# A sorting network on VectorE: every fifth large compare-exchange gets its minimum from integer sums on GpSimd, gathers are issued between the steps, and the closing linear layer runs for four tiles at once on TensorE

## The chip, the cores and the metric

The kernel runs on one core of a Trainium2 chip, in one launch. The metric is the device time of one execution in microseconds (us). One execution was also taken by the hardware profiler; every duration of a single instruction below comes from it.

## What is computed

Two graph layers run one after the other. The first is an attention layer over 4096 nodes and a sparse adjacency matrix; the change doesn't touch it. The second gathers, for every node, the feature rows (128 numbers) of the neighbours that are kept, sorts them feature by feature, takes three quantiles of each feature, and ends in a linear layer:

```python
vals = jnp.where(keep[:, :, None], x[None, :, :], big)
svals = jnp.sort(vals, axis=1)
...
for q in QUANTILES:                       # 0.25, 0.5, 0.75
    idx = jnp.maximum(jnp.ceil(q * n_keep).astype(jnp.int32) - 1, 0)
    picked = jnp.take_along_axis(svals, idx[:, None, None], axis=1)[:, 0, :]
    agg = agg + w_q * picked              # w_q = 1/3
...
agg = 0.5 * agg + 0.5 * x
out = agg @ W.T + b + x
```

## The kernel before

**Two stages.** The first 3850 us are the attention layer (`gat`). Then `sparse` (L1516) does the second layer, and this is the stage that is changed. It goes through 32 tiles of 128 nodes, one node to a partition, ordered by their number of kept neighbours: tile t has `HIGH[t]` = 50 to 100 slots, each a row of 128 float32 of one neighbour.

**One tile.** `load` (L1653) issues from GpSimd's queue (POOL) one indirect DMA for the node's list of neighbours (`info`), one for its own features (`xs`) and one for each slot (`gather`, L1548, whose DMA is L1549), so some 66 for a usual tile. They fill one of three buffers `rows`, so the gathers of tile t+1 can only begin when the quantiles of tile t-2 have been read out of theirs. `plan` (L1500) makes a sorting network for the slots, cut down to the positions that the quantiles need, and `steps` packs equal compare-exchanges into rectangles of at most 16 slots (`PAIRS`), that is 2048 numbers per partition. The network of a tile is done in two halves: the first half beside the second half of the tile before it. `interleave` (L1467) merges the two lists so that neighbouring steps touch different slots.

**One step.** `compare` (L1572) of a step that needs both results copies the low side with ScalarE (ACT) to a tile of PSUM (`low`, two buffers; `low_s` in SBUF for up to four slots), and VectorE (DVE) then writes the minimum over the low side and the maximum over the high side:

```python
nc.scalar.copy(packed, lows)                                     # L1583
nc.vector.tensor_tensor(lows, packed, highs, op=ALU.min)         # L1584
nc.vector.tensor_tensor(highs, packed, highs, op=ALU.max)        # L1585
```

Steps that need one result take one DVE instruction (L1587, L1589).

**The end of a tile.** `finish` (L1591) reads out the three quantiles with weights (L1618 to L1632) into `agg`; the largest tiles have extra slots that are merged here (L1599 to L1614). Then DVE adds `agg` and `xs` and halves them (L1636, L1637), TensorE transposes the tile (L1639), ACT copies it, TensorE multiplies it with the weights (L1642), DVE adds `xs`, the bias and the product (L1644, L1645), and an indirect DMA on POOL's queue writes the tile (L1646).

**What sets the order.** The Tile framework decides where instructions stand on each engine when the program is built; from then on every engine takes its own list strictly in order, and an instruction that waits for a semaphore holds up all behind it. POOL's list in this stage holds nothing but the indirect DMAs.

Of the kernel before, what the change touches and what calls it, by code (L numbers as in the profile page):

```python
# [38 lines left out]
F32 = mybir.dt.float32  # L39
F16 = mybir.dt.float16  # L40
BF = mybir.dt.bfloat16
I32 = mybir.dt.int32
# [3 lines left out]
ALU = mybir.AluOpType  # L46
# [4 lines left out]
P = 128  # L51
N = 4096
D = 128
# [34 lines left out]
MAIN = 64  # L88
PAIRS = 16
SMALL = 4  # L90

BLOCKS = (4, 4, 6, 6, 6, 6)
START = tuple(sum(BLOCKS[:b]) for b in range(len(BLOCKS)))
# [1373 lines left out]
def interleave(jobs):  # L1467


    at, last, now = [0] * len(jobs), {}, 0  # L1470
    left = [list(j) for j in jobs]
    while any(left):
        best = None
        for j, todo in enumerate(left):
            seen = set()
            for i, step in enumerate(todo[:24]):
                if not (step[-1] & seen):
                    since = now - max((last.get((j, x), -9) for x in step[-1]), default=-9)
                    rank = (min(since, 3), -j, -i)
                    if best is None or rank > best[0]:  # L1480
                        best = (rank, j, i)
                seen |= step[-1]
        _, j, i = best
        step = left[j].pop(i)
        for x in step[-1]:
            last[j, x] = now
        now += 1
        yield j, step


def places(t):
# [24 lines left out]
def sparse(tc, nc, c, x1_d, meta_d, order_d, w, b, out):  # L1516


    with tc.tile_pool(name="sp1", bufs=1) as one, tc.tile_pool(
# [3 lines left out]
    ) as psum:  # L1523
        w_sb = one.tile([P, D], F32, name="lw")
        nc.scalar.dma_start(out=w_sb, in_=w)
        bbc = one.tile([P, D], F32, name="lb")
        nc.scalar.dma_start(out=bbc, in_=b.partition_broadcast(P))
        wT = one.tile([P, D], F32, name="lwT")
        it = one.tile([P, 2 * MIDDLE], I32, name="it_p")
        nc.gpsimd.iota(it, pattern=[[1, 2 * MIDDLE]], base=0, channel_multiplier=0)  # L1530
# [4 lines left out]
        for i in range(4):  # L1535
            nc.sync.dma_start(
                out=order[:, ts(i, NT // 4)],
                in_=order_d[ts(i, N // 4), :].rearrange("(t p) c -> p (t c)", p=P),
            )

        def bank():
            return psum.tile([P, PAIRS * D], F32, name="low")
# [5 lines left out]
        def gather(row, info, col):  # L1548
            nc.gpsimd.indirect_dma_start(  # L1549
                out=row,  # L1550
                out_offset=None,
                in_=x1_d,
                in_offset=bass.IndirectOffsetOnAxis(ap=info[:, col : col + 1], axis=0),
            )

        def view(t, at, *dims):

            dims = [[x * D, k] for x, k in dims if k > 1]
            return bass.AP(
                tensor=t.tensor, offset=t.offset + at * D, ap=[list(t.ap[0]), *dims, [1, D]]  # L1560
            )

        def block(t, shape, shift=0):
            s, n2, step2, n, step, run = shape
            dims = [[x * D, k] for x, k in ((step2, n2), (step, n)) if k > 1]
            return bass.AP(
                tensor=t.tensor,
                offset=t.offset + (s + shift) * D,
                ap=[list(t.ap[0]), *dims, [1, run * D]],
            )  # L1570

        def compare(rows, step):  # L1572
            shape, d, low, high, _ = step
            lows, highs = block(rows, shape), block(rows, shape, d)
            if low and high:
                _, n2, _, n, _, run = shape
                k = n2 * n * run
                if k > SMALL:
                    t = bank()
                else:  # L1580
                    t = tp.tile([P, SMALL * D], F32, name="low_s", bufs=4)
                packed = block(t, (0, n2, n * run, n, run, run))
# [3 lines that stand above are left out]
            elif low:  # L1586
                nc.vector.tensor_tensor(lows, lows, highs, op=ALU.min)  # L1587
            else:
                nc.vector.tensor_tensor(highs, lows, highs, op=ALU.max)  # L1589

        def finish(t, rows, xs, info, extra):  # L1591
            agg = tp.tile([P, D], F32, name="agg")
            shift = MIDDLE - HIGH[t] // 2
            for q, (lo, hi) in enumerate(places(t)):
                n = hi - lo + 1
                if extra:
                    cut = one.tile([P, 3 * (80 - MAIN) * D], F32, name="cut")
                    grid = view(cut, 0, (extra, n), (1, extra))
                    nc.vector.tensor_tensor(  # L1599
                        grid,  # L1600
                        view(rows, lo - extra - 1, (1, n), (1, extra)),
                        view(rows, MAIN, (0, n), (1, extra)),
                        op=ALU.max,
                    )
                    m = extra
                    while m > 1:
                        h = m // 2
                        a = view(cut, 0, (extra, n), (1, h))
                        nc.vector.tensor_tensor(
                            a, a, view(cut, m - h, (extra, n), (1, h)), op=ALU.min  # L1610
                        )
                        m -= h
                    best = view(rows, lo - 1, (1, n))
                    nc.vector.tensor_tensor(best, best, view(cut, 0, (extra, n)), op=ALU.min)  # L1614
                if q == 0:
                    begun = False
                weight = tp.tile([P, 8], F32, name="weight", bufs=4)
                nc.vector.tensor_scalar(  # L1618
                    weight[:, :n],
                    iota_p[:, lo + shift : hi + 1 + shift],  # L1620
                    info.bitcast(F32)[:, POS + q : POS + q + 1],
                    third,
                    op0=ALU.is_equal,
                    op1=ALU.mult,
                )
                for i in range(n):
                    v = view(rows, lo - 1 + i)
                    if not begun:
                        nc.vector.tensor_scalar(agg, v, weight[:, i : i + 1], None, op0=ALU.mult)
                        begun = True  # L1630
                    else:
                        nc.vector.scalar_tensor_tensor(  # L1632
                            agg, v, weight[:, i : i + 1], agg, op0=ALU.mult, op1=ALU.add
                        )
            com = tp.tile([P, D], F32, name="com")
            nc.vector.tensor_add(com, agg, xs)  # L1636
            nc.vector.tensor_scalar(com, com, 0.5, None, op0=ALU.mult)  # L1637
            ps = bank()
            nc.tensor.transpose(ps[:, :P], com, c["idf"])  # L1639
            comT = tp.tile([P, P], F32, name="comT")  # L1640
            nc.scalar.copy(comT, ps[:, :P])
            nc.tensor.matmul(ps[:, 512 : 512 + D], comT, wT, start=True, stop=True)  # L1642
            o = tp.tile([P, D], F32, name="o", bufs=4)
            nc.vector.tensor_add(o, xs, bbc)  # L1644
            nc.vector.tensor_add(o, o, ps[:, 512 : 512 + D])  # L1645
            nc.gpsimd.indirect_dma_start(  # L1646
                out=out,
                out_offset=bass.IndirectOffsetOnAxis(ap=info[:, NODE : NODE + 1], axis=0),
                in_=o,
                in_offset=None,  # L1650
            )

        def load(t):  # L1653
            rows = three.tile([P, max(HIGH), D], F32, name="rows")
            xs = three.tile([P, D], F32, name="xs")
            info = three.tile([P, MW], I32, name="info", bufs=4)
            nc.gpsimd.indirect_dma_start(
                out=info,
                out_offset=None,
                in_=meta_d,  # L1660
                in_offset=bass.IndirectOffsetOnAxis(ap=order[:, t : t + 1], axis=0),
            )
            gather(xs, info, NODE)
            for s in range(HIGH[t]):
                gather(rows[:, s, :], info, s)
            return rows, xs, info

        plans = [plan(t) for t in range(NT)]
        held = {0: load(0), 1: load(1)}
        for t in range(NT + 1):  # L1670
            if 0 < t < NT - 1:
                held[t + 1] = load(t + 1)
            jobs = [
                plans[t - 1][1] if t > 0 else [],
                plans[t][0] if t < NT else [],
            ]
            for j, step in interleave(jobs):
                compare(held[t - 1 + j][0], step)
            if t > 0:
                finish(t - 1, *held.pop(t - 1), plans[t - 1][2])  # L1680


def kept(tc, nc, c, adj, kt_d, num, s2):
# [401 lines left out]
```

## Time and profile before

| | |
|---|---|
| median of 11 runs | 8641.98 us (8606.69 to 8652.89) |
| the profiled execution | 8628.19 us, its span 8626.4 us |
| the sorting stage, 3850 to 8575 us of the span | 4725 us |
| in it busy: DVE | 4343.53 us |
| in it busy: POOL | 2145.52 us |
| in it busy: ACT | 1684.47 us |
| in it busy: PE | 39.37 us |

A busy time is the sum over an engine's instructions. Groups of instructions are listed by line, engine, operation and tile, with their count, busy time, mean duration in ns, and the idle time of the engine just before them with what ended it. The timeline lists single instructions with their start.

### The profile page before, as it was taken

To read this page: it belongs to the slowest core of one execution; us is meant where nothing else is said; L and a number is where in the kernel's file an instruction comes from. 1 tells how busy PE (TensorE), PEld (TensorE's weight loads), DVE (VectorE), ACT (ScalarE), POOL (GpSimd) and SP (SyncE) were. 2 spreads that over 40 slices of the span, in tenths; PEclk is the share of its full clock that TensorE was granted. 3 is DMA by queue.
4 is the path that set the end of the run, shared out by engine and by line. 5 is a ranking of instruction groups with operands and counts; after the bars stand their busy time and mean duration, and the time that the engine had idled before them with its cause. 6 is when DMAs were issued, how large, how long until landed. Compare 5 with 4: busy or idle time off the path is not lost. (4 is left out here: it accounts for less than half of the span.)

```text
span 8626.4 us, 29926 instructions
## 1 busy us (share of the span) xinstructions
PE 1162.3 (13%) x5587; PEld 954.8 (11%) x5587; DVE 5920.5 (69%) x9452; ACT 2153.1 (25%) x2120; POOL 4412.7 (51%) x4564
## 2 busy tenths in 40 slices
PE   3122232322233333330000000000000000000000
PEld 1122222212122222220000000000000000000000
DVE  6344544535432222226988999999989999999999
ACT  5011211200000000002333333333333333333333
POOL 1666566555666666656554454453545355453510
PEclk5565656656565665565555555555555555555555
DMA  5232322222122222211111111110111011110100
GB/s 178 45 87 64 80 67 68 79 45 46 44 42 48 50 49 50 49 40 42 35 37 32 27 36 31 29 40 25 38 28 36 22 31 33 27 38 23 36 8 1
DMA packets 222575, 385.09 MB, mean 45 GB/s; under 512 B 121637, under 2 KB 133416, under 8 KB 222376
## 3 DMA queue, kind: packets, MB, share of 16 engines
q0 software_dynamic: 145664, 305.55, 15.2%
q1 hardware_dynamic: 64258, 70.19, 2.7%
q10 hardware_dynamic: 12454, 7.34, 0.3%
q14 instruction: 153, 1.25, 0.1%
q8 instruction: 46, 0.75, 0.0%
HBM read 372.47 MB, written 10.31 MB: 44 GB/s over the span
## 5 line engine op out<-in xcount | busy, mean ns | idle before, releaser
L1549 POOL DMA_INDIRECT rows<-x_d,info x2078 | 2043.1, 983 | 2065.1 <-DVE agg L1632 1049.9
L886 POOL DMA_INDIRECT nb<-xf_d,ids x2250 | 2140.1, 951 | 1285.6 <-issue 655.0
L1583 ACT COPY low<-rows 128x2048 f32<-128x2048 f32 (+9 forms) x1009 | 1548.2, 1551 | 2563.3 <-DVE rows L1585 1711.3
L1584 DVE TENSOR_TENSOR rows<-low,rows 128x2048 f32<-128x2048 f32 (+9 forms) x1009 | 1878.2, 1886 | 208.9 <-issue 92.8
L1585 DVE TENSOR_TENSOR rows<-low,rows 128x2048 f32<-128x2048 f32 (+9 forms) x1009 | 1876.4, 1885 | 4.2 <-DVE rows L1584 1.2
L1008 PE MATMUL ps_z<-spread,nb 128*128 128x128 f32 x4500 | 782.9, 334 | 1375.9 <-issue 591.1
L1008 PEld LDWEIGHTS ps_z<-spread,nb 128*128 128x128 f32 x4500 | 724.5, 245 | 1472.1 <-issue 909.9
L1001 DVE TENSOR_TENSOR spread<-e,ps_small 128x1152 f32<-128x1152 f32 (+4 forms) x312 | 342.6, 1108 | 735.0 <-remote 643.1
L1639 PE MATMUL low<-idf,com 128*128 128x128 f32 x32 | 15.2, 474 | 4716.7 <-issue 2420.3
L1639 PEld LDWEIGHTS low<-idf,com 128*128 128x128 f32 x32 | 5.8, 182 | 4726.1 <-issue 2425.0
L970 ACT ACTIVATE ps_e<-e 128x256 f32<-128x256 f32 (+4 forms) x64 | 26.1, 408 | 1643.2 <-DVE e L962 981.5
L1646 POOL DMA_INDIRECT out<-o,info x32 | 39.8, 1244 | 503.5 <-DVE o L1645 488.8
L182 DVE MAX8 lists<-cand 128x8 f32<-128x176 f32 x416 | 131.4, 334 | 177.1 <-remote 117.3
L1583 ACT COPY low_s<-rows 128x256 f32<-128x256 f32 (+3 forms) x321 | 144.7, 470 | 398.9 <-issue 140.5
L367 ACT ACTIVATE nz<-a_i 128x1024 bf16<-128x1024 int32 x128 | 134.3, 1049 | 369.5 <-remote 287.3
L182 DVE MAX8 k<-key 128x8 f32<-128x256 f32 x416 | 167.8, 415 | 77.2 <-remote 55.0
L950 DVE TENSOR_REDUCE den<-ps_e 128x32 f32<-128x256 f32 (+15 forms) x92 | 30.4, 356 | 236.3 <-ACT ps_e L982 188.2
L900 DVE TENSOR_TENSOR mine<-me,group 128x64 f32<-128x64 f32 x32 | 6.8, 213 | 258.8 <-remote 163.5
L1585 DVE TENSOR_TENSOR rows<-low_s,rows 128x256 f32<-128x256 f32 (+3 forms) x321 | 157.2, 499 | 4.5 <-DVE rows L1584 3.3
L1584 DVE TENSOR_TENSOR rows<-low_s,rows 128x256 f32<-128x256 f32 (+3 forms) x321 | 156.9, 499 | 1.4 <-ACT low_s L1583 0.7
L184 DVE MATCH_REPLACE8 key<-k,key 128x256 f32<-128x256 f32 x384 | 156.4, 409 | 0.0
L962 DVE TENSOR_TENSOR e<-nb,ps_small 128x144 f32<-128x144 f32 (+8 forms) x166 | 39.9, 260 | 164.6 <-DMA nb<-xf_d,ids 152.8
(222 smaller groups left out, 2592.1 us busy)
## 6 DMA issues: line engine op xcount, KB each, us to landing
a_i<-in_adj SPq DMA_DIRECT2D x128, 512.0 KB
nb<-xf_d,ids POOLq DMA_INDIRECT x2250
rows<-x_d,info POOLq DMA_INDIRECT x2078
xf_d<-xf ACTq DMA_DIRECT2D x4, 576.0 KB
xf<-in_x ACTq DMA_DIRECT2D x4, 512.0 KB
meta_d<-rowdata_k SPq DMA_DIRECT2D x4, 324.0 KB
abc_ta<-in_L_gnn_a ACTq DMA_DIRECT2D x2, 512.0 KB
w_ga<-in_L_gnn_W ACTq DMA_DIRECT2D x2, 512.0 KB
```

The lines of the kernel that those rows point to most:

```text
L182: nc.vector.max(out=top, in_=work)
L184: nc.vector.match_replace(out=work, in_to_replace=top, in_values=work, imm_value=gone)
L367: nc.scalar.activation(nz[:, j, :], a_i, AF.Relu, scale=-1.0, accum_out=self.negative[:, k : k + 1],)
L886: gather = nc.gpsimd.indirect_dma_start(out=rows[:, at + i, :], out_offset=None, in_=xf_d, in_offset=bass.IndirectOffsetOnAxis(ap=ids[:, k ...
L962: nc.vector.tensor_tensor(by_group(e, (g, m, r[g], at)), by_group(rows[:, :, D:], (g, m, r[g], k)), of_group(f1, (g, m, r[g], at)), op=ALU ...
L1001: last = nc.vector.tensor_tensor(spread[:, :m], e[:, at : at + m, :].unsqueeze(2).to_broadcast(shape), own.unsqueeze(1).unsqueeze(3).to_br ...
L1008: product = nc.tensor.matmul(ps_z[:, g, :], rows[:, k + i0 + i, :D], spread[:, i].rearrange("p j h -> p (j h)"), start=i0 + i == 0, stop=i ...
L1549: nc.gpsimd.indirect_dma_start(out=row, out_offset=None, in_=x1_d, in_offset=bass.IndirectOffsetOnAxis(ap=info[:, col : col + 1], axis=0),)
L1583: nc.scalar.copy(packed, lows)
L1584: nc.vector.tensor_tensor(lows, packed, highs, op=ALU.min)
L1585: nc.vector.tensor_tensor(highs, packed, highs, op=ALU.max)
L1646: nc.gpsimd.indirect_dma_start(out=out, out_offset=bass.IndirectOffsetOnAxis(ap=info[:, NODE : NODE + 1], axis=0), in_=o, in_offset=None,)
```

## The change

Four things change in `sparse` and in what it calls.

1. `interleave` counts the steps that have at least 12 slots (`SHARED`) and need both results. Every fifth (`EVERY`) is opened with mark 0, stays open while about two other steps (`AHEAD`) are emitted, and is closed with mark 1. The count starts anew for every tile.
2. For such a step `compare` has GpSimd add both sides as 32-bit integers into a tile `sum` (one buffer) when it is opened. When it is closed, ACT copies the low side, DVE writes the maximum over the high side, and GpSimd writes `sum` less the maximum, as integers, over the low side: that is the minimum, bit for bit. DVE does one instruction for such a step, not two.
3. `load` no longer issues its DMAs at once. The loop over the steps asks for one more gather whenever fewer than 1.25 x 100 x (i + 1) / (number of steps) have been issued at step i.
4. The linear layer is done for four tiles together. TensorE forms `0.5*agg + 0.5*xs` transposed by two matrix products per tile, and `xs`, the bias row and the product with the weights by three per tile, all in one of the two PSUM buffers `low`; ACT copies the results. DVE's instructions L1636, L1637, L1644 and L1645 are gone. The extra slots of large tiles are merged in pieces of at most 32.

```diff
+SHARED = 12
+EVERY = 5
+AHEAD = 2
+BEHIND = 2
...
 def interleave(jobs):
-    while any(left):
+    begun, large = [], 0
+    while any(left) or begun:
...
-            seen = set()
+            seen = {x for _, i, step in begun if i == j for x in step[-1]}
...
+        if begun and (best is None or best[0][0] <= 0 or begun[0][0] <= now):
+            _, j, step = begun.pop(0)
+            for x in step[-1]:
+                last[j, x] = now + BEHIND
+            now += 1
+            yield j, step, 1
+            continue
         _, j, i = best
         step = left[j].pop(i)
+        shape, _, low, high, _ = step
+        if low and high and shape[1] * shape[3] * shape[5] >= SHARED:
+            large += 1
+            if large % EVERY == 0:
+                begun.append((now + AHEAD, j, step))
+                yield j, step, 0
+                continue
...
-        def compare(rows, step):
+        def compare(rows, step, how):
...
+            if how is not None:
+                if how == 0:
+                    t = sums[used] = tp.tile([P, PAIRS * D], I32, name="sum", bufs=1)
+                    nc.gpsimd.tensor_tensor(
+                        block(t, (0, n2, n * run, n, run, run)),
+                        lows.bitcast(I32),
+                        highs.bitcast(I32),
+                        op=ALU.add,
+                    )
+                    return
+                t = bank()
+                packed = block(t, (0, n2, n * run, n, run, run))
+                nc.scalar.copy(packed, lows)
+                nc.vector.tensor_tensor(highs, packed, highs, op=ALU.max)
+                nc.gpsimd.tensor_tensor(
+                    lows.bitcast(I32),
+                    block(sums.pop(used), (0, n2, n * run, n, run, run)),
+                    highs.bitcast(I32),
+                    op=ALU.subtract,
+                )
+                return
...
-            com = tp.tile([P, D], F32, name="com")
-            nc.vector.tensor_add(com, agg, xs)
-            nc.vector.tensor_scalar(com, com, 0.5, None, op0=ALU.mult)
+        def finish(xs, agg, infos):
             ps = bank()
-            nc.tensor.transpose(ps[:, :P], com, c["idf"])
...
+            comT_, o_ = ps[:, : FOUR * P], ps[:, FOUR * P : 2 * FOUR * P]
+            for j in range(FOUR):
+                com = comT_[:, ts(j, P)]
+                nc.tensor.matmul(com, agg[:, j, :], half, start=True, stop=False)
+                nc.tensor.matmul(com, xs[:, j, :], half, start=False, stop=True)
+            comT = one.tile([P, FOUR * P], F32, name="comT")
+            nc.scalar.copy(comT, comT_)
+            for j in range(FOUR):
+                to = o_[:, ts(j, D)]
+                nc.tensor.matmul(to, c["idf"], xs[:, j, :], start=True, stop=False)
+                nc.tensor.matmul(to, c["ones"][0:1, :], b_row[:, j, :], start=False, stop=False)
+                nc.tensor.matmul(to, comT[:, ts(j, P)], wT, start=False, stop=True)
...
-            nc.vector.tensor_add(o, xs, bbc)
-            nc.vector.tensor_add(o, o, ps[:, 512 : 512 + D])
+            nc.scalar.copy(o.rearrange("p t d -> p (t d)"), o_)
...
         for t in range(NT + 1):
+            loads = iter(())
             if 0 < t < NT - 1:
                 held[t + 1] = load(t + 1)
+                loads = held[t + 1][2]
...
-            for j, step in interleave(jobs):
-                compare(held[t - 1 + j][0], step)
+            merged = list(interleave(jobs))
+            done = 0
+            for i, (j, step, how) in enumerate(merged):
+                while done * len(merged) < (i + 1) * 1.25 * max(HIGH):
+                    done += 1
+                    next(loads, None)
+                compare(held[t - 1 + j][0], step, how)
+            for _ in loads:
+                pass
             if t > 0:
...
+                quantile(t - 1, rows, info, plans[t - 1][2], agg[:, (t - 1) % FOUR, :])
+                if t % FOUR == 0:
+                    finish(*group.pop((t - 1) // FOUR))
```

In the changed kernel the integer sum is L1612, the maximum of a shared step L1622, the integer difference L1623, a gather L1579, and the ordinary copy, minimum and maximum are L1636, L1637 and L1638.

## The prediction

> **What bounds the kernel now.** I read the busy shares by slices first, then the sorting stage by engine, then the groups, then the timeline of POOL.
>
> ```profile
> DVE  6344544535432222226988999999989999999999
> POOL 1666566555666666656554454453545355453510
> ```
>
> From slice 19 on (the sort) DVE is at nine tenths or more, POOL at about half. For 3850 to 8575 us the windows view gives:
>
> ```profile
> 3850.00:8575.00 4725.00, 39.37 (x93) 21.19 (x93) 4343.53 (x3629) 1684.47 (x1350) 2145.52 (x2174) 0.50 0.12 30
> ```
>
> DVE is busy for 4343.5 of 4725 us. The groups say with what, and what POOL does meanwhile:
>
> ```profile
> L1549 POOL DMA_INDIRECT rows<-x_d,info x2078 | 2043.1, 983 | 2065.1 <-DVE agg L1632 1049.9
> L1583 ACT COPY low<-rows 128x2048 f32<-128x2048 f32 (+9 forms) x1009 | 1548.2, 1551 | 2563.3 <-DVE rows L1585 1711.3
> L1584 DVE TENSOR_TENSOR rows<-low,rows 128x2048 f32<-128x2048 f32 (+9 forms) x1009 | 1878.2, 1886 | 208.9 <-issue 92.8
> L1585 DVE TENSOR_TENSOR rows<-low,rows 128x2048 f32<-128x2048 f32 (+9 forms) x1009 | 1876.4, 1885 | 4.2 <-DVE rows L1584 1.2
> ```
>
> Minimum and maximum are equally dear; DVE hardly waits; POOL waits as long as it works, for DVE to give back a buffer (`agg` is the readout). POOL's timeline shows the beat of one tile:
>
> ```profile
> 6154.31 0.95 POOL L1549 DMA_INDIRECT rows<-x_d,info  x1 [45.23 <-DVE weight L1618]
> 6155.56 0.94 POOL L1549 DMA_INDIRECT xs<-x_d,info  x1 [0.30 <-issue]
> 6156.80 0.94 POOL L1549 DMA_INDIRECT rows<-x_d,info  x1 [0.30 <-issue]
> ...
> 6240.24 0.98 POOL L1646 DMA_INDIRECT out<-o,info  x1 [0.30 <-issue]
> 6242.76 0.96 POOL L1657 DMA_INDIRECT info<-meta_d,order  x1 [1.53 <-DMA out<-o,info]
> 6288.58 0.94 POOL L1549 DMA_INDIRECT rows<-x_d,info  x1 [44.87 <-DVE weight L1618]
> ```
>
> A gather takes 1.25 us of POOL's queue (0.95 and a gap of 0.30, start to start 1.25). The pass begins when the buffer comes free, lasts about 86 us, and 45 us of rest follow: a beat of 134 us (6154.31 to 6288.58). All of it is hidden only because nothing that DVE needs soon stands behind the gathers.
>
> **What goes.** The built program has 135 shared steps: 86 of 2048 elements, 27 of 1792, 12 of 1536, 7 of 1920, 3 of 1664, on average 1936. A minimum of 2048 lasts 2.28 us and its successor starts 2.20 us later, so one of 1936 holds DVE for 2.09 us: 135 x 2.09 = 282 us less. Of the linear layer L1636, L1637, L1644 and L1645 go, 32 each at 0.29, 0.22, 0.29 and 0.28 us: about 33 us. The wait of L1644 for DMAs (78 us, in 8 waits) goes with it. The pieces of 32 in the merge of extra slots add 5 instructions, under 2 us. Together -393 us.
>
> **What comes: the price of a sum.** No row shows an integer sum on GpSimd. The nearest rows of POOL:
>
> ```profile
> masks.py:199 POOL TENSOR_SCALAR_AFFINE_SELECT idf<-idf 128x128 f32<-128x128 f32 x1 | 0.3, 282 | 0.0
> masks.py:197 POOL MEMSET idf<- 128x128 f32 x1 | 0.2, 205 | 0.3 <-POOLq L2070 0.3
> L2070 POOL MEMSET const-float32-1.0<- 128x1 f32 x1 | 0.1, 115 | 0.0
> ```
>
> The fixed part is 115 ns; writing costs (205 - 115) / 127 = 0.71 ns an element, reading and writing (282 - 115) / 127 = 1.31. If writing alone counts, 2048 elements take 1.6 us; if a second operand costs as much as the first pass over again (2.62 ns), 5.5 us. I take one more read at the difference of the two, 0.60: 1.91 ns, 4.0 us. Both ends stay in the range.
>
> The Trainium skill's "GPSIMD Engine Reference", section 3.1, gives 4.497 us for a two-input sum of 2048 float32 on GpSimd and advises VectorE for such work. By that price the forecast below would be some 85 us later; it doesn't change the sign.
>
> **What comes: the order on POOL.** The source asks for gathers a few at a time, but the built order decides, and it is this for the stretch in which tile 17 is gathered:
>
> ```
> sum<-rows 128x2048          L1612
> rows<-sum,rows              L1623
> rows<-x_d gathers x19       L1579   (first one waits for the buffer)
> sum<-rows 128x2048          L1612
> rows<-x_d gathers x5        L1579
> rows<-sum,rows              L1623
> rows<-x_d gathers x40       L1579
> sum<-rows 128x2048          L1612
> rows<-sum,rows              L1623
> sum, rows<-sum, sum, rows<-sum
> ```
>
> The gathers stand in blocks ahead of the sums. The maximum of a shared step overwrites the high side, so DVE waits there for the sum; behind that maximum stands everything else of DVE. From the free buffer to the end of the third sum POOL needs 64 x 1.25 + 3 x 4.0 = 92 us. Up to that maximum DVE's list has 12 instructions of 2048 and 4 of 1024: 12 x 2.20 + 4 x 1.14 = 31 us. So **DVE stands still for 61 us**, in two waits (19 gathers first, 40 later). Before, the same 80 us of gathers ran beside DVE's whole tile.
>
> Counting the other stretches in the same way: blocks of 16 to 23, 5 and 26 to 39 in tiles 3 and 6 to 11 (39 to 49 us uncovered); one block of 51 to 59 in tiles 5 and 12 to 15 (49 to 54 us: 62 x 1.25 + 2 x 4.0 = 86 against 29 to 33 of DVE); 19 to 20, 5 and 40 to 42 in tiles 16 to 20 (57 to 60 us); 46 to 50, 8 or 9 and 10 to 17 in tiles 21 to 28, where the last difference is needed as well (41 to 63 us); about 45 us in the other four. Over the 29 stretches from tile 2 to tile 30 that is 1495 us, 52 us each.
>
> The first tile: its first sum stands behind 104 gathers, then 57 more with the first differences: 161 x 1.25 + 16 = 217 us on POOL, and DVE work behind it, where the first readout used to come 234 us after the stage began. I count +70 us.
>
> **Smaller waits.** Of four shared steps in a tile about two have no gathers ahead: the maximum waits some 2 us for the sum, the next step some 3 us for the difference, and its copy on ACT comes after that. I count 13 us per tile, and 23 where POOL writes out a group, with `info` and `xs` for the next, between a sum and its difference. ACT's waits of today (92.8 + 82.2 us at L1584, 5.5 per tile) are in that: 29 x (15 - 5.5) = +275 us.
>
> **The linear layer on TensorE.** 20 products per group. The pair of L1642 takes 0.80 us in the timeline, so about 16 us per group, beside DVE's work; but one of the two PSUM buffers is held for as long, and the next three steps can't be copied ahead (2 us each): 8 x 6 = 50 us, nothing if these steps are short.
>
> **The sum.** -393 + 1495 + 70 + 275 + 50 = +1497 us on the profiled 8628.19 us: 10,125 us. The median of the runs lies 14 us above the profiled execution, so I say 10,130 us, 17% slower. Six of the eight GpSimd operations of a tile are on the path, so one microsecond more or less for a sum moves the time by 29 x 6 = 174 us: 1.6 us gives 9,710, 5.5 us gives 10,390.
>
> A further cost that no row shows is that DVE and GpSimd may hold each other up. DVE instructions with both operands in SBUF (`low_s`, L1587, L1589, the merges) are about 700 of 4343 us, 16%; if each of the 270 operations lost up to 2 us in that share of cases, that is 0 to 90 us. The Trainium skill's "SBUF — State Buffer", section "Who interferes with whom", says that just these contend with a GpSimd instruction that reads SBUF, and those with one operand in PSUM don't; L1636 to L1638 mostly have one there, which speaks for the low end.
>
> **Rivals.**
> 1. *The forecast*, sums of 3 to 5.5 us: 9,950 to 10,390 us. For it: fixed order, and a pitch of 1.25 us that holds over whole passes. Chance 0.70.
> 2. *Cheap sums*, under 3 us: the gathers alone hold DVE; 9,700 to 9,950 us. For it: the pure write at 0.71 ns. Chance 0.12.
> 3. *Dear sums*, over 5.5 us or with contention: 10,390 to 10,900 us. For it: strided operands and an integer path that no row shows. Chance 0.13.
> 4. *Faster*: the block of gathers does not hold the sums, and DVE's saving comes through. Place: the sum behind the 40 gathers. It decides where POOL's chain fits beside DVE's 31 us: (31 - 12) / 64 = 0.30 us per gather, as if only the gap occupied the queue and sums ran beside the 0.95 us. Then -393 + 275 = -118, about 8,510 us; with the small waits covered too, 8,235. Against it: each gather starts only 0.30 us after the one before has ended. Chance 0.04.
> 5. *No change*, a chance balance: 0.01.
>
> The range is 9,700 to 10,600 us: it takes in both bounds of the sum, leaves out the faster case and the upper end of rival 3. Slower by over 0.2% (about what a measurement of this kernel can tell from no change) has 0.95, faster 0.04, within 0.2% 0.01.
>
> **What will show it.** Right: the sum at about 4 us; DVE waiting before L1622 for POOL about 1,200 to 1,500 us in all, longest waits 20 to 60 us, right behind blocks of gathers; a beat of about 190 us where it was 134; the stage some 6,220 us long, DVE busy there 4,020 us. Wrong: POOL idle while L1622 waits, sums that overlap gathers, or L1622 waiting for ACT and not for POOL.

## The result, and the profile after

The changed kernel takes 10404.8 us (median of 8 runs, 10393.31 to 10413.63) against 8641.98 us before: ratio 1.2044, 95% interval 1.2032 to 1.2056. It is 20.4% slower where 17% was forecast. The profiled execution took 10416.0 us, its span is 10414.2 us: 1788 us more than before, where +1497 was forecast. The attention layer ends at 3849.9 us before and at 3866.3 us now (taken at the first instruction of the sorting stage, the index ramp L1530, now L1558), so 16 us of the growth lie in a layer that didn't change. The sort has grown from 4776.5 to 6547.9 us, by 1771 us.

The busy shares by slices of the changed kernel:

```profile
DVE  5345445344222224665666566567667777678798
POOL 2655655656666656545554545545554445554532
```

DVE, at nine tenths or more all through the sort before, stands at six to seven tenths until the last slices. POOL is at about half as before, so neither engine is full: they wait for each other. The chain that ended last, by engine, says the same:

```profile
DVE 29%; POOL 22%; issue 9%; ACT 2%; PE 1%; DMA 0%; another core or an unknown queue 0%; DVEq 0%; POOLq 0%; ACTq 0%
```

The windows view of the whole sorting stage (PE, PEld, DVE, ACT, POOL busy):

```profile
3866.00:10415.00 6549.00, 91.74 (x320) 72.76 (x320) 4507.56 (x3437) 1698.31 (x1346) 3273.71 (x2445) 0.50 0.09 22
```

The same view of before, for the stage to its end (the prediction shows it to 8575 us):

```profile
3850.00:8627.00 4777.00, 40.64 (x96) 21.88 (x96) 4382.08 (x3694) 1693.23 (x1362) 2146.89 (x2175) 0.50 0.12 30
```

DVE now has 257 instructions fewer, and is busy for 126 us **more**. Hold on to that number: the forecast had 315 us less. The groups:

```profile
L1579 POOL DMA_INDIRECT rows<-x_d,info x2078 | 1988.9, 957 | 800.8 <-issue 614.6
...
L1637 DVE TENSOR_TENSOR rows<-low,rows 128x2048 f32<-128x2048 f32 (+10 forms) x874 | 1591.7, 1845 | 753.8 <-ACT low L1636 404.7
...
L1612 POOL TENSOR_TENSOR sum<-rows 128x2048 int32<-128x2048 int32 (+3 forms) x135 | 581.1, 4304 | 1700.1 <-DVE rows L1638 1693.8
L1622 DVE TENSOR_TENSOR rows<-low,rows 128x2048 f32<-128x2048 f32 (+3 forms) x135 | 292.6, 2167 | 1231.9 <-POOL sum L1612 1230.4
...
L1623 POOL TENSOR_TENSOR rows<-sum,rows 128x2048 int32<-128x2048 int32 (+3 forms) x135 | 606.6, 4494 | 574.8 <-DVE rows L1622 574.1
```

A gather costs what it did, 0.96 us. The line to read first is L1622: 292.6 us of work and 1231.9 us of idle time in front of it, ended by the integer sum in all but 1.5 us. The waits of DVE in the sort (us in all, times, longest):

```profile
DVE rows L1622 <- POOL sum L1612: 1230.4, 51, 56.3
DVE rows L1637 <- ACT low L1636: 404.7, 148, 35.7
DVE rows L1637 <- POOL rows L1623: 283.9, 27, 36.4
```

Only 51 of the 135 shared steps wait at all; a mean of 24 us each is far more than the 4.5 us of a sum. What POOL does meanwhile is in its timeline (start, us) of the stretch in which tile 17 is gathered:

```profile
6685.38 0.95 POOL L1579 DMA_INDIRECT rows<-x_d,info  x1 [9.51 <-DVE weight L1672]
...
6707.89 0.95 POOL L1579 DMA_INDIRECT rows<-x_d,info  x1 [0.31 <-issue]
6708.86 4.51 POOL L1612 TENSOR_TENSOR sum<-rows 128x2048 int32<-128x2048 int32 x1
6713.52 0.96 POOL L1579 DMA_INDIRECT rows<-x_d,info  x1 [0.16 <-issue]
...
6719.50 4.51 POOL L1623 TENSOR_TENSOR rows<-sum,rows 128x2048 int32<-128x2048 int32 x1
6724.17 0.96 POOL L1579 DMA_INDIRECT rows<-x_d,info  x1 [0.16 <-issue]
...
6772.96 0.95 POOL L1579 DMA_INDIRECT rows<-x_d,info  x1 [0.30 <-issue]
6773.93 4.50 POOL L1612 TENSOR_TENSOR sum<-rows 128x2048 int32<-128x2048 int32 x1
6780.83 4.88 POOL L1623 TENSOR_TENSOR rows<-sum,rows 128x2048 int32<-128x2048 int32 x1 [2.40 <-DVE rows L1622]
```

and DVE's, of the same stretch:

```profile
6713.40 2.29 DVE L1622 TENSOR_TENSOR rows<-low,rows 128x2048 f32<-128x2048 f32 x1 [19.24 <-POOL sum L1612]
6724.04 3.42 DVE L1637 TENSOR_TENSOR rows<-low,rows 128x2048 f32<-128x2048 f32 x2 [8.35 <-POOL rows L1623]
...
6747.69 1.22 DVE L1638 TENSOR_TENSOR rows<-low,rows 128x1024 f32<-128x1024 f32 x1
6778.46 2.29 DVE L1622 TENSOR_TENSOR rows<-low,rows 128x2048 f32<-128x2048 f32 x1 [29.55 <-POOL sum L1612]
6780.67 0.68 DVE L1637 TENSOR_TENSOR rows<-low_s,rows 128x512 f32<-128x512 f32 x1
6781.39 4.87 DVE L1638 TENSOR_TENSOR rows<-low_s,rows 128x512 f32<-128x512 f32 x1
```

POOL works from 6685.38 to 6778.43 with no gap longer than some 0.3 us. The later of the two sums shown (the third of the stretch, as the prediction counts them) stands behind 40 gathers, and DVE, which had nothing left to do at 6748.9, waits 29.55 us for it. Note the last two lines for later: two instructions of the same shape, one of 0.68 us and one of 4.87. The second began 0.56 us after POOL's difference (6780.83) and ended 0.55 us after it (6785.71).

### The profile page after: what moved, and what is told of

Read it like the earlier page. It is cut to its first block, busy times and chain, and to the rows that moved or that the text cites. A ratio compares the mean times of both kernels' runs of the same rounds, so it can differ in the third digit from the quotient of the medians.

```text
span 10414.2 us, 30706 instructions
## 1 busy us (share of the span) xinstructions
PE 1206.1 (12%) x5811; PEld 999.7 (10%) x5811; DVE 6048.4 (58%) x9195; ACT 2159.8 (21%) x2108; POOL 5539.1 (53%) x4834
## 4 chain that ended last, share of the span: by engine, by line
DVE 29%; POOL 22%; issue 9%; ACT 2%; PE 1%; DMA 0%; another core or an unknown queue 0%; DVEq 0%; POOLq 0%; ACTq 0%
POOL rows L1579 17%; DVE rows L1637 12%; DVE rows L1638 10%; POOL rows L1623 2%; POOL sum L1612 2%; ACT low L1636 2%; DVE rows L1622 2%; DVE rows L1640 1%; DVE rows L1642 1%; DVE cut L1663 1%; DVE agg L1686 1%; DVE cut L1653 1%; DVE weight L1672 0%; DVE rows L1668 0%; PE low L1704 0%
## 5 line engine op out<-in xcount | busy, mean ns | idle before, releaser
L1579 POOL DMA_INDIRECT rows<-x_d,info x2078 | 1988.9, 957 | 800.8 <-issue 614.6
L1636 ACT COPY low<-rows 128x2048 f32<-128x2048 f32 (+10 forms) x874 | 1313.5, 1517 | 4127.0 <-DVE rows L1638 1530.3
L1637 DVE TENSOR_TENSOR rows<-low,rows 128x2048 f32<-128x2048 f32 (+10 forms) x874 | 1591.7, 1845 | 753.8 <-ACT low L1636 404.7
L1638 DVE TENSOR_TENSOR rows<-low,rows 128x2048 f32<-128x2048 f32 (+10 forms) x874 | 1589.0, 1842 | 5.1
L1612 POOL TENSOR_TENSOR sum<-rows 128x2048 int32<-128x2048 int32 (+3 forms) x135 | 581.1, 4304 | 1700.1 <-DVE rows L1638 1693.8
L1622 DVE TENSOR_TENSOR rows<-low,rows 128x2048 f32<-128x2048 f32 (+3 forms) x135 | 292.6, 2167 | 1231.9 <-POOL sum L1612 1230.4
L1623 POOL TENSOR_TENSOR rows<-sum,rows 128x2048 int32<-128x2048 int32 (+3 forms) x135 | 606.6, 4494 | 574.8 <-DVE rows L1622 574.1
L1696 PE MATMUL low<-half_i,agg 128*128 128x128 f32 x64 | 21.7, 443 | 6434.9 <-DVE rows L1638 6412.3
L1621 ACT COPY low<-rows 128x2048 f32<-128x2048 f32 (+3 forms) x135 | 239.7, 1776 | 232.9 <-DVE rows L1638 211.5
L1637 DVE TENSOR_TENSOR rows<-low_s,rows 128x256 f32<-128x256 f32 (+3 forms) x321 | 283.4, 892 | 1.6 <-issue 0.7
L1636 ACT COPY low_s<-rows 128x256 f32<-128x256 f32 (+3 forms) x321 | 145.7, 470 | 410.3 <-DVE rows L1637 186.2
L1638 DVE TENSOR_TENSOR rows<-low_s,rows 128x256 f32<-128x256 f32 (+3 forms) x321 | 221.2, 698 | 1.3
L1642 DVE TENSOR_TENSOR rows<-rows 128x128 f32<-128x128 f32 (+7 forms) x231 | 169.0, 745 | 9.8 <-POOL rows L1623 8.7
```

Of the source, the lines that this page charges most:

```text
L1579: nc.gpsimd.indirect_dma_start(out=row, out_offset=None, in_=x1_d, in_offset=bass.IndirectOffsetOnAxis(ap=info[:, col : col + 1], axis=0),)
L1612: nc.gpsimd.tensor_tensor(block(t, (0, n2, n * run, n, run, run)), lows.bitcast(I32), highs.bitcast(I32), op=ALU.add,)
L1623: nc.gpsimd.tensor_tensor(lows.bitcast(I32), block(sums.pop(used), (0, n2, n * run, n, run, run)), highs.bitcast(I32), op=ALU.subtract,)
```

## The experiments

Where the text speaks of a kernel's loss or gain, it is against the kernel before as run beside it. Beside no_sums, plain_loads, spread and one_slot_sums the kernel before takes 8012.08 us, as the attention layer ends at 3243 us in all traces of that set; beside small_8 and small_12 it takes 8607.94 us, beside the rest 8615.49. So only differences and ratios are compared between them, or the stage's own length (4776.5 us before). The totals in the expectations are to be read as distances from some 8,640 us. The kernels plain_loads, plain_no_sums, spread, one_slot_sums and at_load have one timed execution each. Two theories stood at the start. **Queue**: the gathers ahead of the sums on POOL's list make the loss. **Price**: the sums themselves are too dear, wherever they stand. A third cost, DVE and GpSimd holding each other up, was open between 0 and 90 us.

### no_sums: only the linear layer and the gathers between steps

```diff
-EVERY = 5
+EVERY = 1 << 30
```

> The changed kernel without any shared step (EVERY set out of reach): gathers between the steps and the linear layer for four tiles stay, every large step has its minimum on VectorE again. Queue theory (the loss is VectorE waiting for sums that stand behind gathers on GpSimd's list): nothing waits for GpSimd any more, 8,560 to 8,620 us, that is 33 us less work on VectorE, 79 us less waiting at the old L1644, some 50 us back for the PSUM buffer that is held. Rival (the moved gathers or the linear layer on TensorE cost the time): over 8,900 us. Price theory (the sums' own duration and their contention with VectorE): the same as the queue theory, since the sums are gone.

7952.87 us, ratio 0.9927 (0.9913 to 0.9940): 59 us faster. Its sorting stage and its one large wait:

```profile
3243.00:7946.00 4703.00, 83.72 (x320) 66.91 (x320) 4361.46 (x3572) 1695.60 (x1346) 2127.52 (x2175) 0.50 0.12 30
```

```profile
DVE rows L1637 <- ACT low L1636: 295.3, 173, 35.4
```

The whole loss comes with the shared steps; the rest of the change is a small gain, 73 us in the stage (4703.1 against 4776.5). Against the kernel before, the waits for ACT at the ordinary minimum have grown. Of the 295 us, 35.4 and 29.6 are the first two waits of the stage, where the kernel before also stands still for 30.5 us (L1584) and 29.5 us (L1644). The other 230 us stand against 92.8 + 82.2, so some 55 us of the gain are paid back there.

### plain_loads: sums kept, no gathers on POOL's queue

Each tile is filled by one DMA of a fixed block (so other rows than the neighbours') from SP's queue:

```diff
-                for s in range(HIGH[t]):
-                    gather(rows[:, s, :], info, s)
-                    yield s
+                nc.sync.dma_start(
+                    out=rows[:, : HIGH[t], :],
+                    in_=bass.AP(
+                        tensor=x1_d.tensor,
+                        offset=x1_d.offset,
+                        ap=[[D, P], [D, HIGH[t]], [1, D]],
+                    ),
+                )
+                yield 0
```

> The changed kernel with its shared steps, but the gathers of a tile's slots are replaced by one plain DMA from SyncE's queue (so that slots hold other rows than the neighbours'); GpSimd's list holds sums, differences and some four DMAs a tile. Queue theory: the wait before the maximum of shared steps falls from 1,230 us to under 350 us, only the short waits of a pair remain, total 8,800 to 9,050 us. Price theory: the sums are as many and as long as before, so the loss stays: over 10,000 us.

8406.04 us, 394 us slower than before. Its waits of DVE:

```profile
DVE rows L1637 <- ACT low L1636: 337.8, 165, 6.5
DVE rows L1622 <- POOL sum L1612: 84.1, 26, 9.4
DVE rows L1637 <- POOL rows L1623: 73.3, 18, 4.6
```

With the gathers away the wait for the sum falls from 1230.4 to 84.1 us. So the price theory doesn't explain the wait. But what is left is not little: 394 us slower, at the upper end of what was expected, and only 84 us of it are waits for a sum.

### plain_no_sums: neither sums nor gathers

Both edits above together.

> The kernel without shared steps and with one plain DMA per tile in place of its gathers (other rows than the neighbours'). It is the floor for the run with plain loads and shared steps: some 70 us under the kernel without sums, because the first tile comes sooner. Queue theory: the run with plain loads stands some 450 us above it, in pair waits and contention, and the remaining loss of the changed kernel is the gathers' place. Price theory: the distance between these two is the whole loss, over 1,500 us.

8454.95 us, 160 us faster than before. So with plain loads the shared steps cost 394 + 160 = 554 us by the totals, and 518 us stage against stage (the rest lies outside the stage), without a slot gather in sight. The windows view of both, from the start of the stage to beyond its end (the busy times are of the whole stage; the lengths of the stage are 5161 and 4642 us):

```profile
3243.00:9000.00 5757.00, 91.70 (x320) 72.70 (x320) 4600.36 (x3437) 1700.14 (x1346) 1292.21 (x367) 0.55 0.06 25
```

```profile
3805.00:9000.00 5195.00, 88.49 (x321) 70.29 (x321) 4359.35 (x3572) 1695.59 (x1351) 93.66 (x99) 0.55 0.07 27
```

The first is with sums: 135 DVE instructions fewer, and 241 us more of DVE work. As 282 us went with the dropped minima, the busy time of the rest grew by about 523 us; 503 of these are instructions that last longer than others of their shape before the change. Of 518 us between the stages, then, 241 are DVE's work and most of the others waits (84 and 73 us for POOL, 101 us more for ACT: 337.8 against 236.5).

### spread: the gathers really between the steps

Gathers, sums and differences are pinned to the order of the source, and the rate follows the size of the tile:

```diff
-            nc.gpsimd.indirect_dma_start(
+            tc.keep_in_program_order(nc.gpsimd.indirect_dma_start(
...
-                    nc.gpsimd.tensor_tensor(
+                    tc.keep_in_program_order(nc.gpsimd.tensor_tensor(
...
-                while done * len(merged) < (i + 1) * 1.25 * max(HIGH):
+                while done * len(merged) < (i + 1) * 1.0 * (HIGH[min(t + 1, NT - 1)] + 2):
```

> The changed kernel with the same gathers, sums and differences, but GpSimd's list is pinned to the order of the source and the gathers are asked for evenly over all steps of a tile (a rate of 1.0 of the tile's own gathers and not 1.25 of 100). Blocks ahead of a sum are 17 to 35 gathers at most and most have 3 to 10. Queue theory: the waits for GpSimd fall by about 700 us, total about 9,650 us (9,450 to 9,850). Price theory: nothing changes in number or length, 10,400 us.

8966.19 us, 954 us slower than before.

```profile
DVE rows L1622 <- POOL sum L1612: 567.5, 42, 56.2
DVE rows L1637 <- ACT low L1636: 415.1, 174, 35.4
DVE rows L1637 <- POOL rows L1623: 162.3, 30, 8.4
```

The same gathers and the same sums in another order on the same queue: the wait for the sum falls by more than half, and the loss from some 1763 to 954 us, within what the queue theory expected. So at least 809 us of the loss hang on the order alone.

### one_slot_sums: short sums, gathers as in the changed kernel

Sum and difference run over one slot of 128 elements; the rest of the low side keeps its old value.

```diff
-                        block(t, (0, n2, n * run, n, run, run)),
-                        lows.bitcast(I32),
-                        highs.bitcast(I32),
+                        t[:, :D],
+                        block(rows, one_slot).bitcast(I32),
+                        block(rows, one_slot, d).bitcast(I32),
...
```

> The changed kernel in which the integer sum and the difference cover one slot of 128 elements and not the whole step (the low side of a shared step is otherwise left as it was). Each takes about 0.4 us and not 4.5; where they stand among the gathers stays. Queue theory: VectorE still waits behind the gathers, some 1,000 us at the maximum of shared steps, total 9,500 to 9,700 us, and VectorE's instructions with two operands in SBUF have their old length. Price theory: the loss goes with the length, under 8,900 us.

8990.08 us, 978 us slower than before. The groups and the waits (lines are two further down here):

```profile
L1625 POOL TENSOR_TENSOR rows<-sum,rows 128x128 int32<-128x128 int32 x135 | 102.1, 756 | 1014.1 <-DVE rows L1623 1013.3
...
L1613 POOL TENSOR_TENSOR sum<-rows 128x128 int32<-128x128 int32 x135 | 64.4, 477 | 1454.1 <-DVE rows L1639 1238.1 <-DVE rows L1640 214.4
```

```profile
DVE rows L1623 <- POOL sum L1613: 726.5, 39, 53.2
...
DVE rows L1639 <- POOL rows L1625: 313.4, 22, 24.3
```

A sum of half a microsecond still costs DVE 18.6 us at each of 39 waits: the place in the list makes the larger part of the wait, the length of the sums at most the rest of the 1230 us. This kernel shows a second thing. The windows view of its sorting stage:

```profile
3244.00:8989.00 5745.00, 88.15 (x320) 70.18 (x320) 4107.95 (x3437) 1694.26 (x1346) 2244.29 (x2445) 0.50 0.10 25
```

With as many DVE instructions as the changed kernel, in the same steps, DVE is busy for 4108 us and not 4508: its instructions have their old length within some 17 us in all, as the queue theory's expectation says. The long sums are what makes them longer.

### at_load: is asking between the steps worth anything?

All gathers of a tile are asked for in `load`, the sums stay.

```diff
-                loads = held[t + 1][2]
+                for _ in held[t + 1][2]:
+                    pass
```

> The changed kernel with its shared steps, but all gathers of a tile are asked for at its load, as in the kernel before, and not between the steps. Queue theory: the built list of GpSimd has the same blocks of gathers ahead of the same sums (5, then 56, then a sum, for example), so the time is that of the changed kernel or up to 60 us more: about 1,760 to 1,830 us over the kernel before. Rival (asking between the steps does spread them and saves time): 200 us or more above the changed kernel.

10433.19 us, 1818 us slower than before and 28 us above the changed kernel's median; its stage is 6595.4 us, 47 us longer than the changed kernel's. The wait for the sum:

```profile
DVE rows L1622 <- POOL sum L1612: 1356.6, 51, 86.5
```

So this part of the change, as written, gives some 30 to 50 us: the source asks for a few gathers at a time, but the built list gathers them again into blocks.

### idle_sums and idle_sets: what GpSimd's work costs DVE beside it

Both have no shared steps. GpSimd instead works, at the two places of each shared step, on a tile that nobody waits for: one integer sum of 2048 elements, or three memsets of as many, which write and do not read.

```diff
+        idle = one.tile([P, PAIRS * D], I32, name="idle")
+        nc.gpsimd.memset(idle, 0)
...
+            if how is not None:
+                for _ in range(1):
+                    tc.keep_in_program_order(nc.gpsimd.tensor_tensor(idle, idle, idle, op=ALU.add))
+                if how == 0:
+                    return
...
```

> The kernel without shared steps, and beside it 270 integer sums of 128x2048 on GpSimd over a tile that nobody else reads or waits for. What remains is what a sum does to VectorE by running. Contention theory (a GpSimd instruction that reads SBUF holds up VectorE instructions with two operands in SBUF): those instructions get longer by 300 to 450 us in all, those with one operand in PSUM keep their length, and the time is 250 to 450 us over the kernel without sums. Rival (the extra busy time of the changed kernel comes from somewhere else, the sums do no harm by running): within 50 us of the kernel without sums.

> As the run with idle sums, but in the place of each sum three memsets of 128x2048, which write SBUF and read nothing and take GpSimd about as long (3 x 1.6 us). If reading is what collides: no VectorE instruction gets longer, and the time is within 30 us of the kernel without sums. If any GpSimd access collides: as with the idle sums, 250 to 450 us more.

With idle sums 8961.54 us, ratio 1.0402 (1.0376 to 1.0428); with idle memsets 8653.69, ratio 1.0048 (1.0029 to 1.0066). Without either, no_sums' ratio would give 0.9927 x 8615.49 = 8552.6 us: so +409 and +101 us. The sorting stage of each, the busy time of DVE third after the length, with sums and with memsets:

```profile
3839.00:8971.00 5132.00, 91.43 (x320) 72.57 (x320) 4695.79 (x3572) 1695.30 (x1346) 3125.80 (x2445) 0.50 0.11 28
```

```profile
3820.00:8661.00 4841.00, 91.12 (x320) 72.35 (x320) 4387.01 (x3572) 1694.17 (x1346) 3626.21 (x2986) 0.50 0.12 30
```

The groups of one DVE shape and of GpSimd's idle work, with sums:

```profile
L1613 POOL TENSOR_TENSOR idle<-idle 128x2048 int32<-128x2048 int32 x270 | 1001.3, 3708 | 14.0
...
L1646 DVE TENSOR_TENSOR rows<-low_s,rows 128x512 f32<-128x512 f32 x113 | 119.2, 1057 | 1.3 <-issue 1.1
```

and with memsets:

```profile
L1613 POOL MEMSET idle<- 128x2048 int32 x810 | 1466.9, 1811 | 29.4
...
L1646 DVE TENSOR_TENSOR rows<-low_s,rows 128x512 f32<-128x512 f32 x113 | 76.9, 682 | 1.9 <-issue 1.0 <-ACT low_s L1645 0.7
```

This minimum, with both operands in SBUF, takes 682 ns beside memsets, which is its time before the change (680), and 1057 ns on average beside sums. Counted over the stage against the mean time of the same shape before, DVE's instructions without an operand in PSUM are 318 us longer beside idle sums, all of it in those that overlap one. Beside memsets the tensor_tensor instructions with two SBUF operands grow by only some 4 us in all, and the quantiles' instructions with one SBUF operand and a scalar column (L1681, L1692) by some 20 us.

The 101 us of the memsets were not expected. In the stage they are 137 us over no_sums (4840 against 4703), of which 26 are DVE's work and 111 idle time; idle sums have 335 and 94. So about 100 us of idle time come with either kind of work. The memsets take 1.81 us each, not 1.6, and keep POOL busier, but ACT's copies wait 90.8 us for gathers, little more than in the kernel before (83.3). Both idle kernels also keep the changed kernel's order of steps, which no_sums doesn't: whether the 100 us come from that order or from GpSimd's work is open. The two compared with each other have the same order, and there DVE's busy time differs by 309 us: that is what sums, which read, cost DVE over memsets, which don't.

### small_8 and small_12: what the part that gains still pays

Built on no_sums: the low side goes to SBUF, not to one of the two PSUM buffers, for up to 8 or 12 slots.

```diff
-SMALL = 4
+SMALL = 12
...
-EVERY = 5
+EVERY = 1 << 30
...
-                    t = tp.tile([P, SMALL * D], F32, name="low_s", bufs=4)
+                    t = tp.tile([P, SMALL * D], F32, name="low_s", bufs=3)
```

> The kernel without sums, in which steps of up to 8 slots (not 4) copy their low side to SBUF, in three buffers, since the tile of sums no longer takes the room. In the run without sums VectorE waits 295 us for ScalarE's copies. If that is for want of a third place beside the two PSUM buffers, about 100 us of it go: 1.9% under the kernel before. If the copies wait for the data (the step before on the same slots), nothing goes: 0.7% under the kernel before, like the run without sums. No sum runs on GpSimd, so the instructions with two operands in SBUF keep their length.

> The same with steps of up to 12 slots copied to SBUF, in three buffers. By want of a place: about 10 us below the run with 8 slots, 2.0% under the kernel before. By data: as the run without sums, 0.7% under.

With 8 slots 8534.0 us, ratio 0.9918 (0.9895 to 0.9940): its runs lie from 8498.5 to 8573.15 us, and the interval doesn't tell it from no_sums. With 12 slots 8502.64 us, ratio 0.9882 (0.9866 to 0.9898), which is 1.2% faster than the kernel before and the lowest ratio of the kernels that do the whole computation. By the sorting stage of the profiled executions 8 slots gain nothing over no_sums (4701.0 against 4703.1 us) and 12 slots 27 us (4676.4). DVE's waits for copies to PSUM in the sort, with 12 slots:

```profile
DVE rows L1637 <- ACT low L1636: 127.3, 39, 43.7
```

This wait has fallen from 295 to 127 us (131 with 8 slots), but DVE's idle time in the stage only from 342 to 314 us (336 with 8): most of it comes back under other names, as waits without a releaser (78.7 us), for `low_s` (24.3 us) and for data at the stage's start (27.4 us). So the 100 us that want of a place would have given did not come. One thing works against a gain: a gather on POOL takes 1151 ns on average with 12 slots in SBUF, 1064 with 8 and 979 in no_sums. How much time that costs was not tried by itself.

## Why the prediction was right, and where it was short

**The mechanism held.** DVE waits before the maximum of a shared step for a sum that stands behind a block of gathers. The wait is 1230 us (1,200 to 1,500 forecast), the longest 56.3 (20 to 60). In tile 17's stretch POOL needs 93.05 us from the free buffer to the end of the third sum (92 forecast), and DVE's waits there come to 19.24 + 8.35 + 1.94 + 29.55 = 59 us (61, though in four waits where two were forecast). The next tile's first gather comes 194.8 us after this one's (190, where 134 stood). plain_loads takes the gathers away and 84 us of the wait are left; spread moves them and it falls by more than half; one_slot_sums shortens the sum and most of the wait stays. The faster case needed POOL to run sums beside gathers; every sum in the trace starts after the gather before it has ended.

**But the time is that of rival 3.** 10,405 us lies above the forecast's own 9,950 to 10,390 and inside the 10,390 to 10,900 of "dear sums, over 5.5 us or with contention", which had a chance of 0.13. The sums were not dear (4.50 us); it was contention. That the range held owes something to luck: its upper part had been left for dear sums, and an error in the other direction took back a good third of what contention added.

**Where the 291 us are** (profiled execution 10416.0 against the 10,125 of the sum; from there to 10,130 the prediction adds 14 us, which makes 10,139). The stage is DVE's busy time plus its idle time, so the miss can be split without a remainder:

| change, us | forecast | measured | miss |
|---|---|---|---|
| DVE busy (-282 minima, -33 linear layer) | -315 | +126 | +441 |
| DVE idle (1495 + 70 + 275 + 50 - 78) | +1812 | +1646 | -166 |
| the attention layer ahead of the stage | 0 | +16 | +16 |
| the whole | +1497 | +1788 | +291 |

**The step that was mis-sized is contention.** The prediction gave it "0 to 90 us", chose nothing, and leaned to the low end because most of L1636 to L1638 have one operand in PSUM. Those indeed cost what they did: the 874 minima, 874 maxima and 135 shared maxima from `low` are within some 2 us in all of their old times, although 201 of them lie beside a sum or a difference. But the others, 16% of DVE's time by the prediction's count, are 407 us longer than the mean of their shape before, and all of the excess lies in instructions that overlap GpSimd's integer work. (28 of the 407 us are in the quantiles' L1672 and L1683, which read one tensor and a scalar column. The other 34 of the 441 us are mostly that DVE's instructions overlap their own neighbours less than before.) The same shape by its own group, before and after:

```profile
L1584 DVE TENSOR_TENSOR rows<-low_s,rows 128x512 f32<-128x512 f32 x113 | 76.9, 680 | 0.7 <-ACT low_s L1583 0.7
```

```profile
L1637 DVE TENSOR_TENSOR rows<-low_s,rows 128x512 f32<-128x512 f32 x113 | 146.0, 1293 | 1.1 <-issue 0.7
```

The prediction's working let each of the 270 operations lose up to 2 us "in that share of cases". Both factors were too small. At 16% some 43 operations would have met such an instruction; 114 of the 270 did, and each of the 114 DVE instructions lost 3.6 us on average, not up to 2. The hold lasts as long as what is left of the operation: the maximum at 6781.39 us above waited out the difference, 4.87 us for 0.68 us of work. In 113 of the 114 cases GpSimd's operation had begun first, and all 114 instructions end after it by their own usual time less 0.12 to 0.21 us. How often the two meet was left to the 16%; in the stretch above the small steps come right after the shared maximum, while the difference runs. 407 / 135 = 3.0 us per shared step, and 503 / 135 = 3.7 in the pair with plain loads: more than the 2.09 us that its dropped minimum saves. So a shared step loses even where no gather is on the queue.

The Trainium skill's "SBUF — State Buffer", section "Who interferes with whom", states just this: a DVE instruction with two SBUF inputs contends with a GpSimd instruction that reads SBUF, not with one that only writes; and the lock is exclusive, so that the one that comes second waits for the other. The pair of idle kernels (1057 against 682 ns) and the 4.87 us agree with it; the prediction quoted the rule and then priced it too low.

**The idle time was forecast 166 us too high.** Two errors of opposite sign are in that. The price of a sum was taken at 4.0 us and is 4.50 us when undisturbed; with the holds, the sum of 2048 elements averages 4.55 us and the difference 4.77:

```profile
L1623 POOL TENSOR_TENSOR rows<-sum,rows 128x2048 int32<-128x2048 int32 x86 | 410.3, 4771 | 365.8 <-DVE rows L1622 365.4
...
L1612 POOL TENSOR_TENSOR sum<-rows 128x2048 int32<-128x2048 int32 x86 | 391.3, 4550 | 1214.8 <-DVE rows L1638 1209.3 <-issue 4.9
```

By the prediction's own 174 us per microsecond that is +90 to +135 us. The Trainium skill's "GPSIMD Engine Reference", section 3.1, with 4.497 us for a float sum, would have been the better price: the undisturbed integer sum took 4.50. Against it, longer DVE instructions fill time in which DVE would otherwise wait for POOL, so the two costs overlap. one_slot_sums speaks for that: there nothing is held, a sum or difference takes 0.62 us on average, and the same rule gives 1812 - 174 x 3.4 = 1220 us more idle time, where 1242 came. That the price and the overlap make up the 166 us between them is still argued; no run has long sums without the holds.

**The other terms.** The linear layer and the wait of L1644 were 33 + 78 us of gain, less 50 for the held buffer: 61 us, and no_sums gained 59 (73 in its stage). That the two agree so well is partly luck: DVE's busy time fell by 21 us and not by 33, and the waits for ACT's copies took back some 55. "Stage 6,220 us, DVE busy there 4,020" became 6548 and 4508: the miss in the busy time is contention. L1622 hardly waited for ACT (1.4 us).

## What to carry to other kernels

Before a short job that somebody waits for is put on an engine that takes its list in order, read what the built list has ahead of it: here 40 gathers of 1.25 us made a sum of 4.5 us cost 30. And work moved to GpSimd to relieve DVE is not free for DVE: weigh the time saved per step against the time by which its neighbours grow, and get that from a run with the same work on a tile that nobody waits for, beside a control in the same order of steps. When a forecast is short, split the stage into busy and idle time of the bounding engine first; it tells at once whether waits or the engine's own work were wrong.

## What the runs showed of the hardware that was not expected

- A hold between GpSimd and DVE lasts for what is left of the operation that came first: 0.68 us became 4.87 us. It works the other way too: the differences average 4.77 us where an undisturbed one takes 4.50.
- Gathers are held as well. In the kernel before, those that run beside a DVE tensor_tensor with two SBUF operands take 1.12 us on average; all others take 0.95, none over 0.97. The longest, 10.76 us from 7001.10 on, spans an unbroken row of such instructions and ends 0.82 us after the last. With 8 and 12 slots in SBUF more gathers run beside such instructions (730 and 913, against 388 in no_sums).
- An integer sum that reads the same tile twice takes 3.61 us for 2048 elements when undisturbed, and a memset of them 1.81 us.
- The attention layer, the same code in all kernels, ends at 3243 us in one set of runs and between 3796 and 3866 us in the others. No run explains it.
